# Moving both layer-3 products of an image's second half to the end of the first score row of the next image

## The chip, the cores and the metric

The kernel runs on one core of one Trainium2 chip. The metric is the device time of a whole execution in microseconds, as the median of several runs. The engines are called PE (TensorE), DVE (VectorE), ACT (ScalarE), POOL (GpSimd) and SP (SyncE, which issues the DMAs here).

## The reference, cut to what matters

Four layers are applied in turn to `x` of 8 images, 512 channels, 32 x 32 pixels (1024 tokens). Layers 0 to 2 are attention blocks with a residual; layer 3 is a convolution with binary weights and binary inputs.

```python
# layer 0: attn = z / largest singular value of z;  x = Wv·(attn·h) + x
# layer 1
h = group_norm(x).reshape(B, C, N)
q = einsum('oc,bcn->bon', wq, h) + bq[None, :, None]      # k, v alike
logits = einsum('bcn,bcm->bnm', q, k) * C ** -0.5
o = einsum('bnm,bcm->bcn', softmax(logits, axis=-1), v)
x = x + (einsum('oc,bcn->bon', wp, o) + bp[None, :, None])
# layer 2: the same kind of block with 128 inner channels and a batch norm at its end
# layer 3
a = sign(x + c(rsign_bias))
Wb = sign(W) * mean(abs(W), axis=1)[:, None]
y = einsum('bchw,oc->bohw', a, Wb)
t = bn_gamma * (y - bn_mean) * rsqrt(bn_var + eps) + bn_beta + x - pr_shift
out = where(t > 0, t, pr_slope * t) + pr_bias
```

## The kernel before, in words

**Images.** After a first stage over all images (layer 0's projections, weights folded together), `fast` is called once for each image, in the order 6, 7, 0, 1, 2, 3, 4, 5. The text calls them image 0 to image 7 by their place in that order. An image's activations lie in `xt`, 128 partitions x 4 channel chunks x 1024 tokens, of which two are held at a time. Tokens are halved: half 0 and half 1 have 512 each.

**Layer 1 by seven products.** The large products of layer 1 are done block-wise with seven instead of eight block products. `seven` (line 333) is a generator: each of its seven steps issues one block product, a *term*, and the work that moves its result out of the bank of PSUM (on ACT at L339, L350 and L366, on DVE at L345 and L347, on POOL at L360), then yields. The terms are, in order, A11·B11, S2·T2, S3·T3, S1·T1, A12·B21, S4·B22 and A22·T4, and A12, S4 and A22 add into the banks of A11, S1 and S3. The S are sums of blocks of the left operand, which `sums_of` makes on DVE with four additions (L314 for S1, L317 for S2, L318 for S3, L319 for S4). `make_u` (line 473) makes the operand `ut` with two such rounds, and its last step calls `sums_of` on it, which writes the tile `us`.

**Scores.** `scores1` (line 516) then makes the scores: four rounds of seven terms, called *rows* here, so 28 steps, k = 0 to 27. On the page the terms are matmuls at L388 with the operands ut,h or us,hs or us,h or ut,hs, four matmul records each. A row's results go into two tiles of the pool `e` (8 buffers), `lo` and `hi`; after the seventh step of a row the remaining exponentials (L531, L532) and the row's part of the sum `esum` (L534, L536, L537) follow.

**Layer 3.** `leave` (line 679) does layer 3 of one half: signs of `xt` into the tile `sg` on ACT (L686), then for each of two pairs of output blocks a product of four 16-bit matmuls (L698) with the packed signs `sw3`, its unpacking (ACT L709, DVE L710 and L711), the batch norm and residual (DVE L719, which reads `xt`), the two branches (ACT L741 and L742, DVE L749) and the output DMA (L753 on SP, 256 KB each). It yields after each pair. Half 0 is done within the image. Half 1 gets only its signs there: the generator is put into the list `rest3`, and its two products are issued among the steps of the next image's `scores1`.

**What else hangs in these steps.** When the generator of `rest3` is found to be at its end, it is dropped and the load of the next image is issued (`load_x`, L139, four DMAs of 512 KB on SP), into the buffer that the finished image had. From then on `chore(2)` advances, at every second call, the power iteration of layer 0 for later images (`chain`, PE at L1029, L1030 and L1060). At k = 8 `entering` issues the load of `f` (L283 on SP), at k = 10 comes `weights0` for a new pair of images (L290), and at k = 13 and 20 `enter` adds layer 0's result into the next image's `xt` (PE L412, DVE L421, L424 and L426). `values1` follows later; some of its additions on DVE (L577) are already done between the scores.

**What sets the order.** Each engine works through a queue whose order is laid down before the launch by the framework: PE's follows the program, while on DVE, ACT and SP a later instruction may stand ahead of an earlier one that was not expected to be ready. Semaphores between the engines are set by the framework. The bank of PSUM of each product comes from a pool of eight.

Of the kernel before, what the change touches and what calls it, by code (L numbers as in the profile page):

```python
# [85 lines left out]
def kernel(  # L86
# [36 lines left out]
    def bank():  # L123
        return psum["bank"].tile([P, HF], F32, tag="bank", name="bank")
# [9 lines left out]
    def load_x(b, split=False):  # L134
        t = xpool.tile([P, CC, N], F32, tag="x", name="xt")
        src = x[b].rearrange("(cc p) n -> p cc n", p=P)
        for cc in range(CC):
            for ns in [half(h) for h in range(NH)] if split and not cc else [slice(0, N)]:
                nc.sync.dma_start(out=t[:, cc, ns], in_=src[:, cc, ns])  # L139
        return t  # L140

    def half(i):
        return bass.ts(i, HF)
# [161 lines left out]
    def quarters_of(t, rows, cols):  # L305

        return [t[:, rows[k], cols[m]] for m in range(2) for k in range(2)]

    def sums_of(a, more, queued=False):

        a11, a12, a21, a22 = a
        s1, s2, s4 = more
        tt = nc.vector.tensor_tensor
        first = tt(s1, a21, a22, ALU.add)  # L314
        if queued:
            tc.keep_in_program_order(first)
        tt(s2, s1, a11, ALU.subtract)  # L317
        tt(a21, a11, a21, ALU.subtract)  # L318
        tt(s4, a12, s2, ALU.subtract)  # L319
        return {"A11": a11, "A12": a12, "A22": a22, "S1": s1, "S2": s2, "S3": a21, "S4": s4}  # L320
# [147 lines left out]
    def split_h(env, ht):  # L468
        hs = env["big"].tile([P, 3, 2, HF], F32, tag="hs", name="hs")
        b = [ht[:, chunks[k], half(n)] for k in range(2) for n in range(2)]  # L470
        return differences_of(b, [hs[:, i] for i in range(3)])
# [44 lines left out]
    def scores1(env, hb, ua, es):  # L516

        scale = float(C) ** -0.5
        esum = env["small"].tile([P, N], F32, tag="esum", name="esum", bufs=1)
        for i in range(NTH):  # L520
            lo, hi = (env["e"].tile([P, N], F32, tag="e", name="e") for _ in range(2))
            es[i], es[NTH + i] = lo, hi
            term = product_of(
                lambda a, b, q, k: hb[b][:, k, bass.ts(i, P)],
                lambda a, b, q, k: ua[a][:, k, :],
            )

            yield from seven(
                term, lo[:, half(0)], hi[:, half(0)], lo[:, half(1)], hi[:, half(1)], exp=scale
            )  # L530
            nc.scalar.activation(lo[:, half(1)], lo[:, half(1)], AF.Exp, scale=scale)  # L531
            nc.scalar.activation(hi, hi, AF.Exp, scale=scale)  # L532
            if i == 0:
                nc.vector.tensor_tensor(esum, lo, hi, ALU.add)  # L534
            else:
                nc.vector.tensor_tensor(esum, esum, lo, ALU.add)  # L536
                nc.vector.tensor_tensor(esum, esum, hi, ALU.add)  # L537
        es.append(esum)
# [255 lines left out]
    def channels(ap):  # L794
        return ap.rearrange("(cc p) n -> p cc n", p=P)
# [70 lines left out]
    def entering(n):  # L866

        b = order[n]
        f = load_f(b)

        def steps():
            while b // 2 not in ready:
                next(behind)
            if b % 2 == 0:
                for i in (b, b + 1):
                    pvs[i] = weights0(i)
            yield
            yield from enter(resident[b], f, pvs.pop(b), 2 if n else CC)

        return steps()  # L880

    rest3 = []
    verdict = []

    def fast(env, n, hb, ua):


        b = order[n]
        xt = resident.pop(b)
        more = n + 1 < B  # L890
        ahead = iter(())
        count = [0]

        def chore(every):
            count[0] += 1
            if count[0] % every == 0:
                next(behind, None)

        es = [None] * NT
        for k, _ in enumerate(scores1(env, hb, ua, es)):  # L900
            if rest3 and k % 2 == 0:
                if next(rest3[0], "end") == "end":
                    rest3.pop()
                    if more and order[n + 1] not in resident:
                        resident[order[n + 1]] = load_x(order[n + 1])
            if n == 0 and k == 2:
                weights["o"] = sums_of(quarters_of(wo, chunks, cols2), [so[:, i] for i in range(3)], True)
            if n == 0 and k == 6:
                tp = quarters_of(sbw["tpg"], chunks, [slice(0, P), slice(P, 2 * P)])
                weights["tp"] = sums_of(tp, [sp[:, i] for i in range(3)], True)  # L910
            if k == 8 and more:
                ahead = entering(n + 1)


            if k in (10, 13, 20, 27):
                next(ahead, None)
            if not rest3 and k not in (13, 14, 15, 20, 21, 22):
                chore(2)
        esum = es.pop()
        vt = env["big"].tile([P, NT, C], F32, tag="uv", name="vt")  # L920
        for k, _ in enumerate(make_v(hb, vt)):
            if k == 3:
                r = inverse_sums(env, esum, n)
            if k == 5:
                next(ahead, None)
            chore(2)
        for _ in ahead:
            pass
        scratch = env["big"].tile([P, 3, N], F32, tag="us", name="scratch")
        got = []  # L930
        steps = iter(())
        for k, _ in enumerate(values1(env, xt, vt, es, r, scratch)):
            chore(2)
            if k == 5 and more:
                nxt = resident[order[n + 1]]
                hb = split_h(env, normal(env, nxt))
        signs = None
        if more:
            steps = make_u(env, hb, got)
        else:  # L940
            signs = unpacked(env)

        def fill(k=1):
            for _ in range(k):
                next(steps, None)

        made = []
        for k, _ in enumerate(project2(env, xt, made)):
            fill(k > 5)
        tt, pt, gt = made  # L950
        es, esum = scores2(env, pt, tt, lambda t: fill(t % 2))
        banks, r = [None, None], None

        def values2(h, ts):
            if banks[h] is None:
                banks[h] = bank()
            for t in ts:
                mm(  # L958
                    out=banks[h],
                    lhsT=gt[:, t, :],  # L960
                    rhs=es[t][:, half(h)],
                    start=t == 0,
                    stop=t == NT - 1,
                )
            if t == NT - 1:
                att = env["small"].tile([P, HF], F32, tag="half_b", name="att")
                nc.vector.tensor_tensor(att, banks[h], r[:, h, :], ALU.mult)
                return att

        dst = channels(out[b])
        fill()
        values2(0, range(0, 2))
        if more:
            r = inverse_sums(env, esum, B + n)
            values2(0, range(2, NTH))
            att = values2(0, range(NTH, NT))
            values2(1, range(0, NTH))
            close2(xt, att, 0)  # L980
            att = values2(1, range(NTH, NT))
            fill()
            for i, _ in enumerate(leave(env, xt, dst, [0])):
                fill(2 * (i % 2))
            close2(xt, att, 1)
            rest3.append(leave(env, xt, dst, [1], stop=True))
            next(rest3[0])
            fill(2)
            for _ in steps:
                pass  # L990
        else:


            r = inverse_rows(env, esum, B + n)
            att = values2(0, range(2, NT))
            values2(1, range(0, 2))
            close2(xt, att, 0)
            values2(1, range(2, 6))
            before, after = leave(env, xt, dst, [0], signs), leave(env, xt, dst, [1], signs)
            count = count_bad(env)  # L1000
            next(count)
            next(before)
            next(before)
            att = values2(1, range(6, NT))
            next(before)
            close2(xt, att, 1)
            for _ in before:
                pass
            next(after)
            next(count)  # L1010
            for _ in after:
                pass

        return hb, got[0] if more else None
# [648 lines left out]
```

## Time and profile before

| | |
|---|---|
| median of 3 runs | 1899.11 us (1899.01 to 1899.49) |
| the profiled execution, its own time | 1899.52 us |
| its span in the profile | 1897.8 us |
| PE busy | 1878.1 us, 99% |
| DVE busy | 1099.0 us, 58% |
| ACT busy | 511.7 us, 27% |
| POOL busy | 224.6 us, 12% |
| mean granted TensorE clock | 0.998 |

The page has the busy time of every engine, the span in 40 slices, the chain of work that ended last, and the costliest groups of instructions. The views of the trace used below are the timeline of one engine (start, duration, engine, line, operation, tiles written and read, number of merged instructions, and in brackets the idle time before it with what ended it), the waits by engine and line, and the table of stages, which gives for each stretch its length and then the busy time of PE, of the weight loads (PEld), of DVE, ACT and POOL, each with the number of instructions in brackets, the granted clock, the share of DMA and GB/s. A duration of a matmul in the timeline reaches past the start of the next one[...]; the distance between starts is what a matmul takes in a row of them. The time of the profiled execution is 1.7 us more than its span.

### The profile page before, as it was taken

What the parts mean: (1) busy time and instruction counts of PE and PEld (TensorE: products, weight loads), DVE (VectorE), ACT (ScalarE), POOL (GpSimd) and SP (SyncE); (2) the same over time, 40 slices, a digit from 0 to 9 for tenths busy, and PEclk for the clock granted to TensorE, in tenths of its full rate; (3) what the DMA queues carried; (4) which work ended last, traced back from release to release, by engine and by line L of the source; (5) the groups of instructions that cost most, each with busy time, mean ns of one, the idle gap of its engine ahead of it and who ended that gap; (6) DMA issues with size and microseconds to landing.
All of it is one profiled execution on the core that took longest, in us unless ns stands there. A gap on an engine that the chain in (4) does not pass through costs nothing.

```text
span 1897.8 us, 16373 instructions
## 1 busy us (share of the span) xinstructions
PE 1878.1 (99%) x6178; PEld 976.4 (51%) x6178; DVE 1099.0 (58%) x1762; ACT 511.7 (27%) x811; POOL 224.6 (12%) x176
## 2 busy tenths in 40 slices
PE   9999999999999999999999999999999999999997
PEld 4366456544745447444645446544645455544653
DVE  3256576457663677438663675357753775466547
ACT  2142222144212432035202421144202521234013
POOL 0000101200121001200121001200130011101121
PEclk9999999999999999999999999999999999999999
DMA  8420000002000110002000110002000200000001
GB/s 320 162 78 6 1 15 4 1 22 78 17 1 1 39 67 12 1 12 89 17 1 0 41 66 12 1 23 78 12 0 12 89 12 0 1 34 22 12 0 47
DMA packets 25203, 66.52 MB, mean 35 GB/s; under 512 B 3552, under 2 KB 4764, under 8 KB 24476
## 3 DMA queue, kind: packets, MB, share of 16 engines
q1 hardware_dynamic: 24188, 64.96, 9.4%
q8 instruction: 51, 0.84, 0.2%
q10 hardware_dynamic: 864, 0.43, 0.1%
q14 instruction: 36, 0.29, 0.0%
q0 software_dynamic: 64, 0.00, 0.0%
HBM read 46.44 MB, written 18.94 MB: 34 GB/s over the span
## 4 chain that ended last, share of the span: by engine, by line
PE 98%; DVE 1%; ACT 0%; issue 0%; DMA 0%; POOL 0%; ACTq 0%; DVEq 0%
PE bank L388 46%; PE bank L557 20%; PE bank L958 6%; PE bank L806 6%; PE bank L1248 5%; PE bank L658 3%; PE bank L675 3%; PE bank L412 2%; PE bank L698 1%; PE wide L1288 1%; PE bank L1029 1%; PE wide L1342 1%; PE bank L1030 1%; PE quad L1142 1%; PE bank L829 0%; PE bank L1060 0%
## 5 line engine op out<-in xcount | busy, mean ns | idle before, releaser
L557 PE MATMUL bank<-e,vt 128*128 128x512 f32 x768 | 334.2, 593 | 0.0
L557 PEld LDWEIGHTS bank<-e,vt 128*128 128x128 f32 x768 | 144.9, 190 | 174.8 <-issue 173.2
L388 PE MATMUL bank<-ut,h 128*128 128x512 f32 x384 | 182.3, 597 | 0.0
L345 DVE TENSOR_TENSOR e<-bank,e 128x512 f32<-128x512 f32 x128 | 87.6, 685 | 80.5 <-PE bank L388 79.8
L388 PE MATMUL bank<-us,hs 128*128 128x512 f32 x256 | 121.5, 597 | 0.5 <-DVE us L317 0.5
L388 PEld LDWEIGHTS bank<-ut,h 128*128 128x128 f32 x384 | 71.4, 190 | 95.6 <-issue 83.7
L958 PE MATMUL bank<-e,tpg 128*128 128x512 f32 x256 | 114.7, 595 | 0.0
L806 PE MATMUL bank<-tpg 128*128 128x512 f32 x256 | 114.6, 592 | 0.0
L813 ACT ACTIVATE e<-bank 128x512 f32<-128x512 f32 x128 | 76.4, 597 | 128.6 <-PE bank L806 128.6
L360 POOL TENSOR_TENSOR e<-e 128x512 f32<-128x512 f32 x32 | 44.3, 1386 | 402.8 <-ACT e L339 135.8
L388 PE MATMUL bank<-wo,h 128*128 128x256 f32 x384 | 91.8, 382 | 0.0
L388 PE MATMUL bank<-h,wu 128*128 128x512 f32 x192 | 90.3, 593 | 0.7 <-ACT ut L350 0.7
L818 DVE TENSOR_TENSOR esum<-esum,e 128x1024 f32<-128x1024 f32 x48 | 58.8, 1225 | 54.9 <-ACT e L813 54.9
L345 DVE TENSOR_TENSOR vt<-bank,vt 128x512 f32<-128x512 f32 x64 | 44.0, 688 | 69.8 <-PE bank L388 69.5
L806 PEld LDWEIGHTS bank<-tpg 128*128 128x128 f32 x256 | 48.6, 190 | 60.7 <-issue 60.5
L958 PEld LDWEIGHTS bank<-e,tpg 128*128 128x128 f32 x256 | 48.1, 190 | 60.4 <-issue 60.3
L360 POOL TENSOR_TENSOR ut<-ut 128x512 f32<-128x512 f32 x16 | 21.8, 1364 | 471.5 <-ACT ut L341 471.5
L388 PEld LDWEIGHTS bank<-wo,h 128*128 128x128 f32 x384 | 71.6, 190 | 11.5 <-issue 2.5
L388 PEld LDWEIGHTS bank<-us,hs 128*128 128x128 f32 x256 | 47.1, 190 | 53.2 <-issue 47.8
L686 ACT ACTIVATE sg<-xt,rb 128x512 f16<-128x512 f32 x64 | 45.3, 718 | 100.7 <-DVE xt L677 97.1
L1248 PE MATMUL bank<-xt,fg 128*64 128x512 f32 x256 | 59.4, 612 | 4.6 <-DMA fg<-in_w_fg 4.6
L658 PEld LDWEIGHTS bank<-tpg,xt 128*128 128x128 f32 x512 | 59.5, 192 | 7.2 <-issue 7.2
(333 smaller groups left out, 2967.3 us busy)
## 6 DMA issues: line engine op xcount, KB each, us to landing
xt<-in_x SPq DMA_DIRECT2D x55, 512.0 KB
out<-both SPq DMA_DIRECT2D x63, 256.0 KB
rfull<-r_dram SPq DMA_DIRECT2D x15, 512.0 KB
f_dram<-f SPq DMA_DIRECT2D x8, 256.0 KB
fb<-f_dram SPq DMA_DIRECT2D x8, 256.0 KB
w<-in_w SPq DMA_DIRECT2D x1, 1024.0 KB
q<-in_w_q SPq DMA_DIRECT2D x1, 1024.0 KB
k<-in_w_k SPq DMA_DIRECT2D x1, 1024.0 KB
```

The costliest lines, as they stand in the source:

```text
L345: nc.vector.tensor_tensor(dst, ps, u, ALU.add)
L360: nc.gpsimd.tensor_tensor(c22, c22, c12, ALU.add)
L388: mm(out=ps[:, q * w : (q + 1) * w], lhsT=lt(ka, kb, q, k), rhs=rhs(ka, kb, q, k), start=first and q == 0 and k == 0, stop=last and k == 1 ...
L557: mm(out=ps, lhsT=a[:, t, bass.ts(r_, P)], rhs=e[t], start=first and t == 0, stop=last and t == NTH - 1, skip_group_check=True,)
L658: mm(out=ps[:, i, :], lhsT=xt[:, cc, bass.ts(4 * h + i, P)], rhs=sbw["tpg"][:, cc, 2 * P : 3 * P], start=cc == 0, stop=cc == CC - 1,)
L675: mm(out=ps, lhsT=sbw["z"][:, bass.ts(oc, P)], rhs=att, start=True, stop=True)
L686: nc.scalar.activation(sg[:, cc, :], xt[:, cc, half(h)], AF.Sign, bias=rb3[:, cc : cc + 1])
L806: mm(out=ps, lhsT=pt[:, 0, bass.ts(t, P)], rhs=tt[:, 0, half(h)], start=True, stop=True,)
L813: nc.scalar.activation(e[:, half(h)], ps, AF.Exp, scale=float(P) ** -0.5)
L818: nc.vector.tensor_tensor(esum, esum, e, ALU.add)
L958: mm(out=banks[h], lhsT=gt[:, t, :], rhs=es[t][:, half(h)], start=t == 0, stop=t == NT - 1,)
L1248: mm(out=banks[i][side(h), :], lhsT=w0[i][:, cc, :], rhs=xt[:, cc, half(h)], start=cc == 0, stop=cc == CC - 1,)
```

## The change

In the loop over the steps of `scores1`, the two products of the previous image's half 1 were issued after steps 0 and 2, and the end of the generator was found at step 4. Now the generator is advanced twice at step 6 and twice at step 7: at step 6, the last of the first row, both products are issued; at step 7, the first of the second row, the first advance finds the end, and the load of the next image is issued there. With that, `chore` is called from step 7 on instead of step 4, in the images that have something in `rest3` (1 to 7).

```diff
         es = [None] * NT
         for k, _ in enumerate(scores1(env, hb, ua, es)):
-            if rest3 and k % 2 == 0:
-                if next(rest3[0], "end") == "end":
+
+            if rest3 and k in (6, 7):
+                for _ in range(2):
+                    done = next(rest3[0], "end") == "end"
+                if done:
                     rest3.pop()
                     if more and order[n + 1] not in resident:
                         resident[order[n + 1]] = load_x(order[n + 1])
```

## The prediction

> **What bounds the kernel now.** I read the page from part 1 to part 4 first.
>
> ```profile
> PE 1878.1 (99%) x6178; PEld 976.4 (51%) x6178; DVE 1099.0 (58%) x1762; ACT 511.7 (27%) x811; POOL 224.6 (12%) x176
> ...
> PE 98%; DVE 1%; ACT 0%; issue 0%; DMA 0%; POOL 0%; ACTq 0%; DVEq 0%
> ```
>
> The first line gives busy times, the second the shares of the chain that ended last. TensorE (PE) is busy for 99% of the span and is 98% of the chain. The change adds and removes no instruction. So it can cost time only where PE comes to wait, and gain only where PE waits now. All of PE's waits in the view of waits sum to about 10 us, 4.6 us of it the first load. There is little to gain.
>
> Next I read PE's timeline where the scores of an image begin, first of image 0, which has no layer-3 work left over from a predecessor, then of image 3, which has.
>
> ```profile
> 211.73 1.88 PE L388 MATMUL bank<-ut,h 128*128 128x512 f32 x4
> 214.14 1.98 PE L388 MATMUL bank<-us,hs 128*128 128x512 f32 x4 [0.53 <-DVE us L317]
> 215.96 0.38 PE L1029 MATMUL bank<-gm 128*128 128x128 f32 x2
> ...
> 868.32 1.88 PE L388 MATMUL bank<-ut,h 128*128 128x512 f32 x4
> 870.03 1.03 PE L698 MATMUL bank<-sg,sw 128*128 128x512 f16 x4
> 870.92 1.98 PE L388 MATMUL bank<-us,hs 128*128 128x512 f32 x4
> 872.74 1.88 PE L388 MATMUL bank<-ut,h 128*128 128x512 f32 x4
> 874.46 1.03 PE L698 MATMUL bank<-sg,sw 128*128 128x512 f16 x4
> ```
>
> Columns are start, duration, engine, line, operation and tiles; rows start 1.72 us apart, since the printed durations overlap. In image 0 the first term (ut,h) is followed by 0.53 us of waiting for the sum that VectorE makes at L317, the operand of the second term (us,hs). In image 3 the same place holds the first layer-3 product (L698), and the second term starts at 870.92 with no wait shown. VectorE's timeline there:
>
> ```profile
> 868.99 0.74 DVE L347 SCALAR_TENSOR_TENSOR ut<-bank,bu,ut 128x512 f32<-128x512 f32 x1
> 869.65 1.22 DVE L317 TENSOR_TENSOR us<-us,ut 128x1024 f32<-128x1024 f32 x1
> 870.78 1.22 DVE L318 TENSOR_TENSOR ut<-ut 128x1024 f32<-128x1024 f32 x1
> ```
>
> L317 ends at 869.65 + 1.22 = 870.87, 0.05 us before the second term starts. The product of 870.03 to 870.89 (four matmuls, each half of 0.43) sits exactly on that wait.
>
> **What the skill says.** "PSUM — Partial Sum Buffer", section "Engine vs sequencer instructions": matmuls start and complete in program order, and VectorE, ScalarE and GpSimd are strict queues. The trace agrees: in image 0 the products at L1029 stand behind the waiting term and do not pass it. "TensorE: Matmul & The Clock Gate", "What's actually happening": the clock halves after an idle window of about 3.4 us. A wait under 1 us should not do that; the granted clock was 1.00 in every stage that I asked for, and no run shows a longer gap here. "SBUF — State Buffer", "Who interferes with whom": VectorE and GpSimd share a port pair as an exclusive lock. The trace fits: two L719 took 2.42 to 2.44 us together (one 1.77) while GpSimd's L360 ran, 1.41 otherwise.
>
> **The change, part by part.**
>
> *The first product leaves step 0.* Its 0.86 us covered a wait, and the wait stays: L317 follows L347, L314, L347 of the previous stage, none of which is touched, and PE takes its work in program order. I difference the second term's start and the first product's start in all seven images with leftover work: 0.89, 0.88, 0.89, 0.89, 0.89, 0.89, 0.89. This time becomes idle. The product itself needs 0.86 us in its new place, as the second product takes now (874.46 to 875.32). Net 7 x 0.86 = **+6.0 us**. As a lower bound, image 0 stands at 214.14 - (211.73 + 1.72) = 0.69 us, so 7 x 0.69 = 4.8. The upper bound is 7 x 0.89 = 6.2.
>
> *The second product leaves step 2.* What followed it (S1·T1) needs a sum from L314, long done. It covered nothing; it costs its 0.86 us elsewhere: 0.
>
> *Both run back to back after step 6.* Their operand (sg) and two banks are free by then: 0 on PE. All that trails them moves from the first row into the second. Per image VectorE does L710 x2 (0.85), L711 x2 (1.36), L719 x4 (3.84) and L749 x4 (2.95), 9.0 us; ScalarE L709 x2, L741 x4, L742 x4 (1.4 + 2.9 + 3.1), 7.4 us. The table of stages, for rows one, two and three of image 3:
>
> ```profile
> 868.00:882.20 14.20, 14.20 (x39) 6.06 (x38) 14.03 (x18) 7.36 (x12) 1.78 (x1) 1.00 0.07 25
> 882.20:895.50 13.30, 13.30 (x33) 5.34 (x31) 6.68 (x10) 5.52 (x9) 1.27 (x1) 1.00 0.59 214
> 895.50:909.60 14.10, 14.10 (x37) 5.93 (x36) 10.69 (x17) 3.43 (x6) 1.27 (x1) 1.00 0.00 1
> ```
>
> The numbers after the length are PE, weight loads, VectorE, ScalarE, GpSimd. VectorE is full in row one today (14.03 of 14.20) and half idle in row two (6.68 of 13.30). After, row two lasts 13.30 + 1.72 = 15.0 and VectorE has 6.68 + 9.0 - 1.46 (two L749 already there) = 14.2. It fits with 0.8 us to spare, and then meets row three, where `enter` keeps it solid from 896.72 to 906. The tightest point there: the S3 product's eviction (L345) ends at 905.34 + 0.69 = 906.03, and A22·T4 into the same bank starts at 907.88, so a backlog of over 1.85 us is needed before PE stops. On ScalarE the tight one is the move of S1·T1 before S4·B22 1.72 us later: in row one of image 1, amid layer-3 work, it ended at 440.72 + 0.57 = 441.29, 0.18 us before PE's 441.47. The same crowd now sits in row two; one more 0.8 us activation ahead of it would cost 0.6. I take +0.1 per image for both, **+0.7**, between 0 (no row stops PE today) and 1.5 per image (0.6 there and a backlog of about 2.8 at the other).
>
> *The load of the next image and the output DMAs.* SP sends four 256 KB outputs, and four 512 KB loads that wait for the last L719, which reads xt. In image 3 the first product's end moves from 870.89 to 882.19 (11.3 later), the second's from 875.32 to 883.05 (7.7 later). The last L719 ended at 880.97, the loads were issued from 881.06 and moved data until about 890.4, 9.4 us. Add 7.7: the last lands at about 898, the first two chunks near 894. `enter` reads the first chunk at 896.72 + 0.86 = 897.6, the last two not before 910.8. So 0, with 3 us spare; images without L290 (1.06 us) have 2 to 2.5. If late, VectorE waits, and the 1.85 us above is what guards PE. The outputs free two e buffers near 896 that row four takes after 911; sg's goes to row three. The f load (L283, at 911.74) behind them on SP is not moved.
>
> *The chores.* They start once the leftover is gone, so at step 7 instead of 4: in images 1 and 2, 21 steps of the power-iteration chain instead of 23. Before, 25 + 23 = 48 of 66 are done after image 1, and image 2 needs 18 of 23. After, 25 + 21 = 46, and it needs 20 of 21. The same PE work, no deadline missed: 0, within 0.3 either way, since chain steps stay two terms apart.
>
> *What could be gained.* Row one takes 882.19 - 868.32 = 13.87 us, where seven terms and two products at 1.72 and 0.86 take 13.73. Even if all 0.14 went, that is 1 us over seven images; it is the start of PE on a late semaphore, which stays. I take 0.
>
> **Sum.** 6.0 + 0.7 = 6.7. The profiled execution took 1899.52 (span 1897.8, 1.7 around it), so 1906.2 against its own time. The median of runs is 0.41 lower: 1899.11 + 6.7 = **1905.8 us**.
>
> **The rivals.** A change of 0.2% (3.8 us) is about what a measurement can tell from none.
>
> *A. The uncovered wait, rows else intact* (forecast): +4.8 to +8. Chance 0.70.
>
> *B. Row two jams as well.* VectorE at 14.2 of 15.0 us, port collisions included, or a late ScalarE move stops PE each time. For it: that fill level, and `enter` right behind. Against: eight banks, and row one stands the same crowd today without a stop. With 0.3 to 1.5 us per image, +8 to +17, 1907 to 1916. Chance 0.18.
>
> *C. The wait closes by itself: not slower.* Place: VectorE's order before L317. L317 does not use what the second L347 writes; were it put ahead (0.66 us earlier), 0.86 - 0.66 = 0.2 us would remain per image, +1.4, 1900.5. It decides once L317 ends 0.32 us earlier (0.54 x 7 = 3.8). Against: image 0 has the same order with PE standing idle, so nothing there reacts to the idleness. Or PE gets other work in the hole, if the product isn't really moved in its queue; L698's place will tell. Chance 0.10.
>
> *D. A gain* from a relieved row one: at most 1 us by the 0.14 above, more only where the chores' shift removes chain waits. Chance 0.02 of over 0.2%.
>
> **Numbers.** Slower 0.88 (A, B), same 0.10, faster 0.02. The low end, 1902.6, takes half of the cover (3.5 us) and leaves out C; the high end, 1913.0, takes in most of B.
>
> **What would show it.** In the profile after, a wait of PE at L388 for L317 seven times at about 0.85, eight with image 0, some 6.5 us in all; L698 in pairs 1.72 us long just before the second row's first term; VectorE near 6.5 of 13.3 us in row one and over 90% in row two; the loads 7 to 8 us later, with no wait of VectorE for xt. Wrong if PE's waits for L317 stay at one, or if PE waits in rows two and three for VectorE or ScalarE by more than 2 us in all.

## The result, and the profile after

| | before | after |
|---|---|---|
| median, runs of one chip (6 each) | 1899.07 us | 1906.41 us (1905.79 to 1906.86) |
| ratio, over all runs | | 1.0038, 95% interval 1.0028 to 1.0048 |
| the profiled execution, its own time | 1899.52 us | 1905.95 us |
| its span | 1897.8 us | 1904.2 us |

The kernel is slower by 7.3 us; 1905.8 was forecast. First parts 1 and 4 of the page after, busy times and shares of the chain that ended last:

```profile
PE 1879.2 (99%) x6178; PEld 976.3 (51%) x6178; DVE 1094.4 (57%) x1762; ACT 511.3 (27%) x811; POOL 221.2 (12%) x176
...
PE 92%; DVE 6%; ACT 1%; issue 1%; DMA 0%; POOL 0%; ACTq 0%; DVEq 0%
```

PE's share is 99% as before, and DVE is even busy for 4.6 us less. In the chain DVE's part goes from 1% to 6%. That points to a wait for DVE but does not price it: 5% of the span is some 95 us, and only about 7 were lost, since the chain, once it has crossed to DVE, is followed back along DVE's own work. Next the waits of PE (what waited and for what: us in total, times, longest), the first line of before and the others of after:

```profile
PE bank L388 <- DVE us L317: 0.5, 1, 0.5
...
PE bank L388 <- DVE us L317: 5.8, 8, 0.9
PE bank L1251 <- DMA fg<-in_w_fg: 4.5, 1, 4.5
PE bank L388 <- ACT ut L350: 0.7, 1, 0.7
```

L388 waited for L317 once before, for 0.5 us; now it waits in every image. PE's and DVE's timelines at image 3, the place that the prediction shows of before:

```profile
869.23 1.88 PE L388 MATMUL bank<-ut,h 128*128 128x512 f32 x4
871.99 1.98 PE L388 MATMUL bank<-us,hs 128*128 128x512 f32 x4 [0.89 <-DVE us L317]
873.81 1.88 PE L388 MATMUL bank<-ut,h 128*128 128x512 f32 x4
...
880.68 1.88 PE L388 MATMUL bank<-ut,hs 128*128 128x512 f32 x4
882.40 1.89 PE L698 MATMUL bank<-sg,sw 128*128 128x512 f16 x8
884.12 1.88 PE L388 MATMUL bank<-ut,h 128*128 128x512 f32 x4
```

```profile
870.07 0.74 DVE L347 SCALAR_TENSOR_TENSOR ut<-bank,bu,ut 128x512 f32<-128x512 f32 x1
870.73 1.21 DVE L317 TENSOR_TENSOR us<-us,ut 128x1024 f32<-128x1024 f32 x1
```

L317 ends at 870.73 + 1.21 = 871.94, and the second term starts 0.05 us later, as before. Between the first term and it there is nothing now. The two products stand as a pair of eight matmuls from 882.40 to 884.12, 1.72 us, ahead of the second row. From the start of the first term to that of the second it takes 2.60 to 2.61 us in images 1 to 7 before, with the product inside, and 2.60 to 2.62 after, without it (2.76 in image 3). Where nothing waits it is 1.72. So each hole is 0.89 us (1.04 in image 3), though the bracket of the usual image prints only 0.73 (0.89 in image 3). The Trainium skill, "Perfetto Trace Analysis", section "Tensor Engine Instruction (MATMUL, LD_WEIGHTS)", says that the end of a matmul in a profile is estimated, not observed. This trace agrees: a term is printed 1.88 us long with the next 1.72 us behind it, so the printed wait is 0.16 short, and holes are measured below from start to start.

The table of stages for rows one, two and three of image 3 (length, then PE, weight loads, DVE, ACT, POOL):

```profile
869.20:882.40 13.20, 12.31 (x30) 5.15 (x29) 7.00 (x8) 2.49 (x4) 1.26 (x1) 1.00 0.00 1
882.40:897.50 15.10, 15.10 (x43) 6.23 (x41) 12.17 (x19) 10.50 (x17) 1.55 (x1) 1.00 0.41 138
897.50:911.60 14.10, 14.10 (x37) 5.92 (x36) 10.69 (x17) 3.42 (x6) 1.26 (x1) 1.00 0.19 77
```

By these busy times PE loses 0.89 us in row one, the printed wait of image 3, and nothing in rows two and three. DVE has changed places: 7.00 of 13.20 us in row one, 12.17 of 15.10 in row two.

To give every microsecond its place I took the length of each image from PE's timelines, from the start of its first score term to that of the next image (for image 7, to the end of PE's last matmul):

| image | 0 | 1 | 2 | 3 | 4 | 5 | 6 | 7 | sum of differences |
|---|---|---|---|---|---|---|---|---|---|
| before | 219.30 | 220.50 | 216.79 | 208.88 | 207.63 | 208.89 | 207.64 | 185.88 | |
| after | 219.31 | 220.47 | 218.62 | 209.91 | 208.76 | 209.75 | 208.77 | 187.01 | +7.09 |

Image 5 costs 0.86, the bare hole. Images 4, 6 and 7 cost 1.13 each, 0.26 to 0.27 more, and image 3 costs 0.17 more, as its hole is 0.15 longer. Images 1 and 2 together cost +1.80, two holes and 0.07, but unevenly. The stage ahead of image 0, which the change does not touch, varied by about 1 us between profiled executions; the spans therefore differ by only 6.4.

What images 4, 6 and 7 have and image 5 does not have is seen at the end of row two. First PE, then ACT, in image 4:

```profile
1100.74 1.88 PE L388 MATMUL bank<-ut,h 128*128 128x512 f32 x4
1102.46 1.02 PE L388 MATMUL bank<-ut,hs 128*128 128x512 f32 x2
1103.48 1.98 PE L388 MATMUL bank<-us,h 128*128 128x512 f32 x4
1105.30 1.02 PE L388 MATMUL bank<-ut,hs 128*128 128x512 f32 x2
```

```profile
1101.46 1.51 ACT L742 ACTIVATE both<-both,pb,ct 128x512 f32<-128x512 f32 x2
1102.87 0.56 ACT L339 COPY e<-bank 128x512 f32<-128x512 f32 x1
```

S4·B22 (us,h) needs the bank that L339 empties of S1·T1. L339 stands behind layer 3's activations on ACT and ends at 1102.87 + 0.56 = 1103.43, 0.05 us before S4·B22 starts, and so it does in images 6 and 7. Half of A22·T4 (ut,hs x2) stands ahead of S4·B22 in PE's queue and fills 1102.46 to 1103.32. The wait that is left is 1103.48 - 1103.32 = 0.16 us, and the start of PE after it costs 1.82 - 1.72 = 0.10 more: together 0.26. So PE's queue does not always follow the order in which `seven` issues its terms, as the section on the kernel said; at this place half of a later term was put forward. At step 0 nothing was.

### The profile page after: what moved, and what is told of

Read it like the earlier page. It is cut to its first block, busy times and chain, and to the rows that moved or that the text cites. A ratio compares the mean times of both kernels' runs of the same rounds, so it can differ in the third digit from the quotient of the medians.

```text
span 1904.2 us, 16397 instructions
## 1 busy us (share of the span) xinstructions
PE 1879.2 (99%) x6178; PEld 976.3 (51%) x6178; DVE 1094.4 (57%) x1762; ACT 511.3 (27%) x811; POOL 221.2 (12%) x176
## 4 chain that ended last, share of the span: by engine, by line
PE 92%; DVE 6%; ACT 1%; issue 1%; DMA 0%; POOL 0%; ACTq 0%; DVEq 0%
PE bank L388 42%; PE bank L557 20%; PE bank L961 6%; PE bank L806 6%; PE bank L1251 5%; PE bank L658 3%; PE bank L412 2%; PE bank L675 2%; PE wide L1291 1%; DVE both L749 1%; PE bank L698 1%; DVE both L719 1%; PE bank L1032 1%; PE wide L1345 1%; PE bank L1033 1%; DVE xt L677 1%
## 5 line engine op out<-in xcount | busy, mean ns | idle before, releaser
L388 PE MATMUL bank<-ut,h 128*128 128x512 f32 x384 | 182.4, 597 | 0.0
L388 PE MATMUL bank<-us,hs 128*128 128x512 f32 x256 | 121.2, 596 | 5.8 <-DVE us L317 5.8
L388 PEld LDWEIGHTS bank<-ut,h 128*128 128x128 f32 x384 | 70.9, 190 | 89.2 <-issue 77.2
L388 PE MATMUL bank<-wo,h 128*128 128x256 f32 x384 | 92.2, 383 | 0.0
L388 PE MATMUL bank<-h,wu 128*128 128x512 f32 x192 | 90.3, 593 | 0.7 <-ACT ut L350 0.7
L360 POOL TENSOR_TENSOR e<-e 128x512 f32<-128x512 f32 x32 | 42.3, 1322 | 410.9 <-ACT e L339 211.7
L388 PEld LDWEIGHTS bank<-us,hs 128*128 128x128 f32 x256 | 47.7, 190 | 67.9 <-issue 54.1
L388 PEld LDWEIGHTS bank<-wo,h 128*128 128x128 f32 x384 | 71.2, 190 | 12.1 <-issue 3.4
L360 POOL TENSOR_TENSOR ut<-ut 128x512 f32<-128x512 f32 x16 | 21.8, 1364 | 471.5 <-ACT ut L341 471.5
```

The lines of the kernel that those rows point to most:

```text
L360: nc.gpsimd.tensor_tensor(c22, c22, c12, ALU.add)
L388: mm(out=ps[:, q * w : (q + 1) * w], lhsT=lt(ka, kb, q, k), rhs=rhs(ka, kb, q, k), start=first and q == 0 and k == 0, stop=last and k == 1 ...
```

## The experiments

All experiments change the steps at which the generator of `rest3` is advanced, or the order of the additions behind L317. Each median is to be compared with that of the kernel before on the same chip: 1899.09 us for the first four, 1899.48 for the other four. The ratios are taken over all runs and can differ in the last digit from those of the medians. An "image length" is a length as in the table above, and a sum of them is against the kernel before.

**Both products after step 2.** The hole at step 0 stays open, and row two gets no layer-3 work.

```diff
-            if rest3 and k in (6, 7):
-                for _ in range(2):
+            if rest3 and k in (2, 4):
+                for _ in range({2: 2, 4: 1}[k]):
```

> Both products are issued after step 2 and the end is found at step 4 as before, so that layer 3's trailing work stays in row one, the load and the chores start where they did, and only step 0 loses its product. Theory W: PE waits for L317 in every image, some 6 us in all, and the time is +6.0 us (5.5 to 6.5) over the kernel before, that is about 1 us less than the changed kernel, which pays for row two as well. Rival R: +0 to +1 us.

Measured: 1905.60 us, ratio 1.0032 (1.0020 to 1.0044). PE's wait for L317 and its timeline at image 3:

```profile
PE bank L388 <- DVE us L317: 5.6, 8, 0.7
```

```profile
869.59 1.88 PE L388 MATMUL bank<-ut,h 128*128 128x512 f32 x4
872.20 1.98 PE L388 MATMUL bank<-us,hs 128*128 128x512 f32 x4 [0.73 <-DVE us L317]
```

The median is 6.5 us above before, at the upper end of what was expected. The image lengths sum to +6.35, and images 2 to 7 cost 0.85 to 0.88 each, 0.867 in the mean. Image 1 costs 1.14; there a small product of the power iteration (L1063, which needs L1059 of DVE) starts 0.40 instead of 0.22 us after the one ahead of it, and the term after it 0.24 instead of 0.14 after that, together 0.28, the excess of this image. So most of the loss comes with the product's leaving step 0, here as in the changed kernel. Seven bare holes are 7 x 0.867 = 6.07, which leaves about 1 us of the 7.09 for what else happens in the changed kernel.

**The first product back after step 0, the second left after step 6.** The cover is restored, and row two has half of its layer-3 work.

```diff
-            if rest3 and k in (6, 7):
-                for _ in range(2):
+            if rest3 and k in (0, 6, 7):
+                for _ in range({0: 1, 6: 1, 7: 1}[k]):
```

> The first product is back at step 0, the second comes at step 6, the end of the generator (with the load and the chores) stays at step 7. Theory W (the changed kernel loses the 0.86 us per image that the first product covered at step 0): PE's waits for L317 are back at one (0.5 us), and the time is that of the kernel before, +0 to +0.8 us (half of the layer-3 work and the late load still sit in row two). Rival R (the second row's crowd on DVE and ACT, or the late load and chores, cost the 7 us): half or more of it stays, +3.5 us or more.

Measured: 1900.14 us, ratio 1.0005 (0.9997 to 1.0013); image lengths +1.16. PE's wait for L317 is back at one, of 0.5 us. The rest is a split of A22·T4 of the kind shown above, now in row one of all seven images with leftover work, as here in image 5:

```profile
1294.09 1.02 PE L388 MATMUL bank<-ut,hs 128*128 128x512 f32 x2
1295.01 1.98 PE L388 MATMUL bank<-us,h 128*128 128x512 f32 x4
```

S4·B22 starts 0.92 us after the half term, not 0.86, and with the 0.10 of the start that is 0.16 an image, 1.1 us in seven. In each of them S4·B22 starts 0.05 to 0.06 us after L339 ends. With the first product back, 5.9 of the 7.1 us are gone, and these seven splits are nearly all of the 1.16 that are left; they put the median 1.05 us above before, a little over the 0.8 that was expected. The loads are late here too (the first of image 3 is issued at 886.93, before at 881.06), so late loads cost next to nothing.

**The products in their old places, the end found at step 7.** Only the chores come later.

```diff
-            if rest3 and k in (6, 7):
-                for _ in range(2):
+            if rest3 and k in (0, 2, 7):
+                for _ in range({0: 1, 2: 1, 7: 1}[k]):
```

> The products stay at steps 0 and 2 as in the kernel before; only the end of the generator is found at step 7 instead of 4, so that the load of the next image and the chores start later. Theory W: no difference from the kernel before, within 0.5 us. Rival R in the form of the late load or the shifted chores: +1 us or more, up to 7.

Measured: 1899.40 us, ratio 1.0000 (0.9991 to 1.0008); image lengths +0.02. Image 1 is shorter by 0.89 us and image 2 longer by 0.89: two steps of the power iteration move from the one to the other. That explains why images 1 and 2 of the changed kernel differ so. The loads hardly moved here (the first of image 3 issued at 881.15 instead of 881.06, since it waits for the last L719 anyway), so this run says nothing of late loads; the one before it does.

**L317 earlier, on the changed kernel.** The three additions are issued ahead of the second L347, which none of them needs; S4, which needs it, follows.

```diff
         term(pd, "A22", "T4", False, True)
-        plus(vd, b2, c21, c21)
+        with tc.issue_after(early().ins):      # S1, S2, S3 here
+            plus(vd, b2, c21, c21)
         if then is not None:
             then()                             # S4 here
```

The diff is cut: `early` is a new function in `make_u` that makes the three sums, and `then` now makes S4 alone.

> The changed kernel, with the sums for the scores in another order on DVE: S1, S2 and S3 are made before the eviction of make_u's last term (L347), which only S4 needs, so that S2 comes 0.66 us earlier. Theory W: PE's wait at step 0 falls from 0.89 to about 0.23 us in each of images 1 to 7 and from 0.69 to about 0.1 in image 0; the time falls by 0.66 x 8 = 5.3 us against the changed kernel, to +1.5 to +2.5 us over the kernel before. Rival R: within 0.5 us of the changed kernel, +7 us.

Measured: 1902.42 us, ratio 1.0016 (1.0010 to 1.0023) against before, 4.0 us less than the changed kernel. That is 3.3 us over before, and so less of a gain than was expected (5.3, to +1.5 to +2.5). The lines show DVE and PE of this kernel at image 3, where L488 to L490 and L498 are the four additions, L489 that of S2, and L392 is the line of the terms:

```profile
868.28 1.23 DVE L488 TENSOR_TENSOR us<-ut 128x1024 f32<-128x1024 f32 x1
869.61 1.23 DVE L489 TENSOR_TENSOR us<-us,ut 128x1024 f32<-128x1024 f32 x1
870.75 1.22 DVE L490 TENSOR_TENSOR ut<-ut 128x1024 f32<-128x1024 f32 x1
871.89 0.74 DVE L347 SCALAR_TENSOR_TENSOR ut<-bank,bu,ut 128x512 f32<-128x512 f32 x1
```

```profile
868.59 1.88 PE L392 MATMUL bank<-ut,h 128*128 128x512 f32 x4
870.89 1.98 PE L392 MATMUL bank<-us,hs 128*128 128x512 f32 x4 [0.42 <-DVE us L489]
```

L489 ends at 870.84, and PE starts 0.05 us later: the time follows this addition. The gap from first to second term is 2.14 instead of 2.61 us in the usual image, 0.47 less, and all eight image lengths fell by 0.45 to 0.47, 3.7 in all. Of the 0.66 that L347 takes, 0.19 did not arrive: L489 reads what L488 has just written and starts 1.33 us after it, while an addition that needs nothing of its immediate predecessor (L490) starts 1.14 after one of the same length.

**Both products after step 0.** The cover is doubled, and all layer-3 work falls into row one.

```diff
-            if rest3 and k in (6, 7):
-                for _ in range(2):
+            if rest3 and k in (0, 4):
+                for _ in range({0: 2, 4: 1}[k]):
```

> Both products are issued after step 0, the end is found at step 4 as in the kernel before. Theory W: the wait of 0.89 us there is covered as it is by one product, the second product costs its 0.86 us wherever it stands; so the time of the kernel before, 0 to -0.9 us (PE then never starts on a late sum, 0.13 us an image). Rival: the second product at step 2 covered something as well, then +1 us or more, up to +6.

Measured: 1901.82 us, ratio 1.0013 (1.0006 to 1.0020); image lengths +2.60, 0.41 to 0.44 in images 3 to 7. The expectation (0 to -0.9) failed, and the number lies where the rival put it, though not for the rival's reason, as the waits show. The waits for L317 are back at one. A new wait stands in the list; it is shown first, and then its place on PE in image 4:

```profile
PE bank L388 <- ACT e L339: 1.2, 5, 0.2
```

```profile
1090.08 1.08 PE L388 MATMUL bank<-ut,hs 128*128 128x512 f32 x2
1091.39 1.99 PE L388 MATMUL bank<-us,h 128*128 128x512 f32 x4 [0.23 <-ACT e L339]
1093.21 1.02 PE L388 MATMUL bank<-ut,hs 128*128 128x512 f32 x2
```

The second term is now free of waiting: it follows the pair without a gap. But with both products ahead of the same row, ACT has too many activations in front of L339, and S4·B22 is 1091.39 - 1090.08 - 0.86 = 0.45 us late, with 0.10 for the start. Against before, PE no longer starts late at the second term (1.72 instead of 1.82 to the third, and 0.03 ahead of it), so about 0.43 is left. Nothing waits at step 2, where the second product stood before, so it had covered nothing there. Cover beyond the wait buys nothing, and the crowd on ACT costs where it meets S4·B22.

**Both products after step 5.** If the splits in row two of images 4, 6 and 7 come from layer 3's activations standing just ahead of L339, a start one step earlier should remove them.

```diff
-            if rest3 and k in (6, 7):
-                for _ in range(2):
+            if rest3 and k in (5, 7):
+                for _ in range({5: 2, 7: 1}[k]):
```

> Both products one step earlier than in the changed kernel, after step 5, the end still at step 7: the cover is gone as there, but the activations of layer 3 reach ACT before the move of row two's S1·T1 is due, and PE's queue has no split A22·T4 in images 4, 6 and 7. Theory W with the late move as the second cost: step 0 costs 0.87 us in each of the seven images and the 0.26 us in images 4, 6 and 7 go, 0.5 to 1.0 us less than the changed kernel, +5.8 to +6.6 us over the kernel before. Rival (the 0.26 us has to do with the late load or with DVE): no less than the changed kernel.

Measured: 1906.57 us, ratio 1.0035 (1.0021 to 1.0049). This is 7.1 us over before, so the time of the whole is not below that of the changed kernel, as the rival had it. The splits, however, are gone, and images 4, 6 and 7 take 208.52, 208.50 and 186.77 us, 0.24 to 0.27 less each than after. PE and ACT in image 4:

```profile
1103.73 1.90 PE L388 MATMUL bank<-us,h 128*128 128x512 f32 x4
```

```profile
1103.04 0.56 ACT L339 COPY e<-bank 128x512 f32<-128x512 f32 x1
```

L339 now ends at 1103.60, 0.13 us before S4·B22, which no longer waits. The load is as late as in the changed kernel, so it was not the cause of these 0.26 us; that is the second mechanism, and its size. Images 1 and 2 became 0.29 and 0.15 us longer: in each a product of the power iteration (L1063 and L1032) starts late, so the image lengths fall by only 0.3 in all. PE waits for L317 for 5.8 us in eight places, as in the changed kernel.

**L317 earlier, on the kernel before.** The same edit as on the changed kernel. There the product covers the wait, so only image 0 has something to gain.

> The kernel before with the reordered sums of the previous experiment (S1, S2 and S3 ahead of the last L347). Theory W: S2 then comes 0.47 us earlier, as the reordered changed kernel showed (2.14 instead of 2.61 us after the first term's start), which is inside the first product's cover in images 1 to 7, so that only what PE still loses there goes (0.03 to 0.13 us each), and image 0 gains 0.47: -0.7 to -1.4 us against the kernel before. Rival: PE loses nothing there before, -0.5 us at most, all of it in image 0.

Measured: 1899.00 us, ratio 0.9999 (0.9990 to 1.0007); image lengths +0.05. The expected gain of 0.7 or more did not come; in its place stands the rival's, at most 0.5 and all of it in image 0, which gains 0.46 us, though PE did lose something there before. In images 1 to 7 the second term starts 0.03 earlier and no longer waits, so the third starts 0.13 earlier, but together they lose 0.5. PE (A12·B21, S4·B22 and A22·T4 of row one) and then ACT in image 4 show where:

```profile
1084.50 1.88 PE L392 MATMUL bank<-ut,h 128*128 128x512 f32 x4
1086.30 1.98 PE L392 MATMUL bank<-us,h 128*128 128x512 f32 x4
1088.12 1.88 PE L392 MATMUL bank<-ut,hs 128*128 128x512 f32 x4
```

```profile
1085.68 0.57 ACT L339 COPY e<-bank 128x512 f32<-128x512 f32 x1
```

The distances are 1.80 and 1.82 instead of 1.72 each. L339 ends at 1086.25, and S4·B22 starts 0.05 us later; in all seven images it follows L339 so. In the kernel before, L339 ended 0.18 us ahead of it. PE now comes 0.13 earlier, the move on ACT 0.07 to 0.08 later, and PE waits for it and pays the 0.10 of the start: what was won at L317 is lost at L339. Image 3 loses most (0.21), as L339 comes another 0.15 later there.

**The same, and a step of the power iteration after step 0 of image 0.** It fills the hole that image 0 has.

```diff
-        count = [0]
+        count = [0 if n else 1]
```

> The same, and in image 0 the first step of the power iteration is issued after step 0 instead of step 1, so that the hole there is covered too (0.58 us of small products where 0.22 us of waiting is left). Theory W: 0.2 to 0.4 us less than without it, -1.0 to -1.8 us against the kernel before. Rival: the hole in image 0 is not on the path, no difference.

Measured: 1898.67 us, ratio 0.9998 (0.9989 to 1.0006); image lengths -0.29, of which image 0 gives -0.80. That is 0.3 us less than without it, as expected, but only 0.8 less than before, where 1.0 or more was expected. No version beats the kernel before by more than a measurement of it can tell.

## Why the prediction was right, point by point

- **The first product leaves step 0: +6.0, measured +6.07** (7 x 0.867, the mean cost of images 2 to 7 with both products after step 2). Removing the cover gave 6.35, with 0.28 of the power iteration in it; bringing it back took 5.9 away; moving L317 moved the time with it, 0.47 us an image. The wait is shown to be the cause. The lower bound of 4.8 from image 0 was too low: in the images with leftover work the hole is the whole 0.89, less the 0.03 that the start had cost before. In image 0 DVE stands idle before the L347 ahead of L314, which starts 1.45 us before the first term (210.28); in the usual later image it stands behind L677 and starts 1.23 to 1.24 before it, and L317 with it 0.20 later. Image 0 was the same code, but not with the same work ahead of it.
- **The second product leaves step 2: 0.** It covered nothing, as said. In the changed kernel no wait follows at step 2, and with both products there that step cost nothing beyond the hole at step 0.
- **Both products after step 6: +0.7, measured about 0.8 in another form.** The term was made of ScalarE and VectorE together, at 0.1 an image; that its size fits is in part luck. VectorE's part was 0, and the step that failed is its fill: 12.17 of 15.10 us, 81%, where over 90% was forecast. Layer 3 took 7.6 us there instead of 9.0, which is 1.4 of the 2.0 us that are missing, mostly because the four L719 took 2.73 us instead of the 3.84 that the prediction took from row one. That price had the overlap with GpSimd's L360 in it; in row two of image 3 the four L719 are over by 889.72, and L360 runs from 893.75. VectorE even stood idle before the last evictions of the row (1.18 and 0.95 us), so no backlog reached row three. ScalarE's part was the move of S1·T1, as named, but in three images of 0.26 us rather than in all: 0.78. In images 3 and 5 L290's work (1.06 us) stands between S1·T1 and S4·B22, and they lose nothing there. The 0.15 of image 3 belongs to its hole at step 0: the L347 behind L677 starts 1.10 instead of 1.24 us before the first term. Why is open; the experiments with the earlier sums on the changed kernel and with both products after step 5 show it as well, the one with both after step 2 doesn't.
- **Loads and outputs: 0, confirmed.** The first load of image 3 is issued at 889.87 instead of 881.06. Of these 8.8 us, 0.9 is the later start of the image; the other 7.9 were forecast as 7.7. At the chunk that `enter` reads first, L421 waits for PE's own L412 (0.36 us, as before), not for the load.
- **Chores: 0, within 0.3.** The experiment on the chores alone moved 0.89 us from image 1 to image 2 and nothing in the sum. That they can cost about 0.3 where they meet other work shows in image 1 with both products after step 2 or 5.
- **A gain: taken as 0, and none found.** The late start of PE in row one, which was to stay, did go with the earlier sums on the kernel before, and L339 took the gain back. Two figures of this part were a little high: the 0.14 of row one is 0.03 and 0.10 of a late start, and the waits of PE before sum to 8.5 us in the view, not to 10. Nothing rests on either.
- **The sum.** 6.7 forecast, 7.09 in the image lengths, 7.3 in the medians. The 0.2 between the last two is less than the 1.07 us by which the runs of the changed kernel differ.
- **The rivals.** A happened, with 0.8 us of the ScalarE half of B. C did not: L317 kept its place behind L347, and the products moved in PE's queue as written. Its price of 0.66 us an image would also have been too high: the experiment with the earlier addition got 0.47.
- **What would show it.** Eight waits for L317, the pair of products of 1.72 us, the later loads and row one's fill came as described. The printed total of 5.8 us missed the announced 6.5, since a printed wait is 0.16 shorter than its hole. The test on rows two and three (under 2 us of waits) held, with 0.8.
- **The order on PE.** The prediction took from the Trainium skill, "PSUM — Partial Sum Buffer", section "Engine vs sequencer instructions", that matmuls start in program order, and read it as the order in which the kernel issues its terms. At step 0 that came true. In row two of images 4, 6 and 7 half of A22·T4 started ahead of S4·B22, which is issued before it. The traces show only the starts, so that the framework laid the queue down in this order, and the chip kept to it, is inferred from that page and not shown here.

## What to carry to other kernels

Moving an instruction changes nothing in the amount of work, and yet it can cost the whole duration of that instruction, where this had filled the wait for a late operand. Before moving it, look at a copy of the same code without it (here image 0), difference the starts around it, and look whether the copy has the same work ahead of the late operand. A wait taken away is won only as far as the next one allows: here L339 had only 0.18 us to spare. Then ask what trails the moved work on the other engines, and which single eviction that crowd will stand in front of, rather than how full the engine is. Take the price of a trailing instruction from a place without collisions, if it goes to such a place.

## What was not expected of the hardware

- A term that waited for its operand costs about 0.10 us on top of the wait: the next term starts 1.82 us after it, not 1.72, in the kernels before and after and in the experiments. With the wait gone (both products after step 0, or the earlier sums on the kernel before) it is 1.71 to 1.73. What makes it isn't shown, and 1.82 also stands where no wait is printed, as after L290 in image 3 of the changed kernel (892.14 to 893.96).
- The Trainium skill, "VectorE: DVE Perf Modes", section "The DRAIN you can't avoid", says of eight copies in a row that a semaphore after each costs nothing extra. No run here has such copies. For these additions of 128 x 1024 elements, reading the immediate predecessor's result does cost: the next one starts 1.13 to 1.15 us after its predecessor where it needs nothing of it, 1.32 to 1.33 where it reads its result (L488 and L489), and 1.26 at another such pair of before (L327 and L328, at 187.96 and 189.22). The 0.19 is what was missing in the experiment with the earlier addition; whether a semaphore makes it isn't shown.
- VectorE was busy for 4.6 us less and GpSimd for 3.4 us less in the slower kernel. Of VectorE's part L719 gives more than the whole: its 56 instructions took 39.4 instead of 47.1 us, none longer than 0.75 us, where before some took up to 1.77 us (in image 3 beside L360). It was worth nothing, since neither was the bound there.
